# A graph-network kernel on five engines: issuing every engine's work in the kernel's own list order instead of the framework's own order

## The chip, the cores and the metric

The kernel runs on one core of a Trainium2 chip. The metric is the device time of one execution in microseconds (us), the median of several. Five engines take part: TensorE (PE in the profile; its weight loads are PEld), VectorE (DVE), ScalarE (ACT), GpSimd (POOL) and SyncE (SP), which issues the transfers. The profile lists each engine's instructions apart (in the kernel before 7664 on TensorE, 3479 on VectorE, 1802 on ScalarE, 519 on GpSimd), and shows for an engine's idle time the operation of another engine, or the transfer, that ended it (18.0 us of TensorE's ended with the gate L465 on ScalarE).

## The reference

A batch of 64 graphs with 256 nodes and 128 features, one 256x256 adjacency `adj`, float32. Four layers, each followed by a residual and a layer normalization. Cut to what matters:

```python
# layer 0: five steps of a gated recurrence (m_in = m_out because both matrices are adj)
def step(h):
    m = einsum('nm,bmd->bnd', adj, h);  av = concat([m, m]);  u3 = h @ u3_w.T + u3_b
    z = sigmoid(av @ w3_w.T + w3_b + u3)
    r = sigmoid(av @ w4_w.T + w4_b + u3)
    hv = tanh(av @ w5_w.T + w5_b + (r * h @ u5_w.T + u5_b))
    return (1 - z) * h + z * hv
# layer 1: edge values in a softmax (the same for all graphs), then adj-like @ (x @ W)
# layer 2: attention: softmax of scores per graph, masked by adj; then an MLP with two normalizations and relus
# layer 3: Chebyshev sums adj @ x, adj @ adj @ x with seven weights
x = layernorm(x + layer_k(x, adj))      # for k = 0..3
```

## The kernel before

Two graphs form a pair, there are 32 pairs, and each passes through a long chain of small dependent operations. To keep TensorE busy, the kernel weaves the chains of several pairs together: in the 1500 us of the middle TensorE is 95% busy, in the last 182 us, where few pairs are left, 78%. It does this with a scheduler of its own, written in Python and run while the program is built. Each operation is noted with the engine (or two possible engines), a duration, and what it reads and writes:

```python
SEEN = {"PE": 0.3, "ACT": 0.15, "DVE": 0.15, "POOL": 0.2, "SP": 2.5}   # the list's own figures: us until others see the end
DUE, LAST_DUE, LAST = 50.0, 10.0, 7                                   # pairs become due every 50 us, the last 7 every 10
...
def pool(us, fn, r, w):
    S.add([("POOL", us, fn)], r, w)
...
# Schedule.order: always the operation that can start first; among equals the most urgent pair
key = (start + (us if len(op.ways) > 1 else 0.0), self.due(op.pair) - op.rest, op.number)
...
return [(op, fn) for _, _, op, fn in sorted(out, key=lambda x: x[:2])]
```

I call the result the **list order**. It also decides which buffer each value gets. There are two sorts of operations in it. The *chain* of the recurrence sits between matmuls of the same pair:

```python
act(0.69, ... nc.scalar.activation(r, t, AF.Tanh, ...))       # L465, first gate; L471 and L479 are its sisters
dve(0.74, ... nc.vector.scalar_tensor_tensor(r, r, 1.0, hT))  # L467
dve(0.76, ...)  # L481     dve(0.74, ...)  # L482     dve(0.72, ... new state)  # L484
evacuate(...)   # L180 on ACT or L181 on DVE: a finished PSUM bank to SBUF
```

The *side work* comes from layers 1 to 3 and the normalizations of all layers. Some of it is four instructions under one entry of the list:

```python
def stats(y):                                   # bn_stats x4, bn_aggr x4 on DVE (L426, L428): 1.75
    pool(0.23, ... add eps)  # L431/L433        pool(1.04, ... pow -0.5)  # L434
    dve(0.16, ...)                              # L436: -mean * rstd
def normalize(y, o):                            # four ACT (L447, 1.85) or four DVE (L442, 1.45) instructions
...
for c in range(4): act(0.51, ... AF.Prelu)      # L550, softmax scores
for c in range(4): act(0.69, ... AF.Exp)        # L553, with a sum
pool(1.3, ... hg + gat_b)                       # L573
act-or-dve(0.62 / 0.8, ... Relu)                # L574
```

At the end of the kernel the list is emitted, one call after the other. In the kernel before, the framework receives these calls and schedules them again: it may give each engine another order, as long as data dependencies hold.

Of the kernel before, what the change touches and what calls it, by code (L numbers as in the profile page):

```python
# [153 lines left out]
def kernel(ctx: ExitStack, tc: tile.TileContext, x, xT, adj, adjT, mats, cols, rows, out):  # L154
# [6 lines left out]
    S = Schedule(n_pairs)  # L161
# [468 lines left out]
    tiles = {}  # L630
    for cls, (n, count) in CLASSES.items():
        where = {"PS": psum, "D": dram}.get(cls, shared)
        tiles[cls] = [where.tile([1, n] if cls == "D" else [P, n], F32, name=f"{cls.lower()}{k}") for k in range(count)]
    for op, fn in S.order(tiles):
        for v, ap in op.tiles.items():
            v.ap = ap
        fn()


# [39 lines left out]
```

## Time and profile before

| | before |
|---|---|
| time, median of 3 | 1832.84 us (1828.77 to 1836.44) |
| profiled span, mean TensorE clock | 1831.8 us, 0.986 |

What TensorE needs if it never waits is worked out in the prediction: about 1656 us. What lies above that is waiting, and time in which the granted clock was 0.50 (47.8 us of it fall within the matmuls). The views that the prediction reads are shown there. A list of waits shows for which operation of which other engine an engine stood still. The columns of a list of waits are the line that waited, the line waited for, then the total in us, how often, and the longest.

```profile
ACT a L574 <- POOL a L573: 80.8, 25, 4.6
ACT a L447 <- DVE s L436: 66.2, 33, 6.6
ACT x L447 <- DVE s L436: 62.2, 33, 5.1
ACT b L550 <- DVE s L542: 33.3, 24, 3.4
```

ScalarE stood 242.5 us (the sum of the four) in front of side work that was not ready.

### The profile page before, as it was taken

What the parts mean: (1) busy time and instruction counts of PE and PEld (TensorE: products, weight loads), DVE (VectorE), ACT (ScalarE), POOL (GpSimd) and SP (SyncE); (2) the same over time, 40 slices, a digit from 0 to 9 for tenths busy, and PEclk for the clock granted to TensorE, in tenths of its full rate; (3) what the DMA queues carried; (4) which work ended last, traced back from release to release, by engine and by line L of the source; (5) the groups of instructions that cost most, each with busy time, mean ns of one, the idle gap of its engine ahead of it and who ended that gap; (6) DMA issues with size and microseconds to landing.
All of it is one profiled execution on the core that took longest, in us unless ns stands there. A gap on an engine that the chain in (4) does not pass through costs nothing. (4 is left out here: it accounts for less than half of the span.)

```text
span 1831.8 us, 22230 instructions
## 1 busy us (share of the span) xinstructions
PE 1707.2 (93%) x7664; PEld 1197.9 (65%) x7664; DVE 1158.6 (63%) x3479; ACT 870.2 (48%) x1802; POOL 442.8 (24%) x519
## 2 busy tenths in 40 slices
PE   8999999999999899999998999999899999998886
PEld 5666667666766566766666666676665666666775
DVE  5467657567566656565665665666666665766764
ACT  3445344545455544444555453454453445444653
POOL 0013112212231312221232221222212220215342
PEclk9999999999999999999999999999999999999999
DMA  5000000010001000000000001001000000000000
GB/s 148 6 12 12 18 24 18 18 30 12 18 24 29 1 30 18 24 12 23 12 23 18 18 18 29 18 18 27 3 18 12 17 13 1 6 18 6 13 24 24
DMA packets 48978, 37.36 MB, mean 20 GB/s; under 512 B 2912, under 2 KB 44384, under 8 KB 48864
## 3 DMA queue, kind: packets, MB, share of 16 engines
q1 hardware_dynamic: 48864, 35.93, 6.7%
q8 instruction: 60, 0.98, 0.2%
q14 instruction: 54, 0.44, 0.1%
HBM read 27.47 MB, written 8.45 MB: 20 GB/s over the span
## 5 line engine op out<-in xcount | busy, mean ns | idle before, releaser
L180 ACT COPY a<-ps 128x512 f32<-128x512 f32 (+1 forms) x508 | 267.4, 537 | 346.9 <-PE ps L412 210.3
L431 POOL TENSOR_SCALAR s<-s 128x4 f32<-128x4 f32 x160 | 52.0, 325 | 1018.0 <-DVE s L428 949.5
L412 PE MATMUL ps<-aT,a 128*128 128x256 f32 x1024 | 250.0, 384 | 6.9 <-ACT a L180 6.5
L412 PEld LDWEIGHTS ps<-aT,a 128*128 128x128 f32 x1024 | 189.8, 192 | 59.6 <-issue 23.3
L434 POOL TENSOR_TENSOR s<-s,neg_half 128x4 f32<-128x4 f32 x192 | 204.7, 1066 | 15.8
L469 PE MATMUL ps<-a,w 128*128 128x512 f32 x320 | 165.5, 605 | 18.0 <-ACT a L465 18.0
L479 ACT ACTIVATE a<-ps,bzrh 128x512 f32<-128x512 f32 x160 | 109.3, 684 | 144.2 <-PE ps L477 142.9
L426 DVE BATCH_NORM_STATS2 s<-a 128x6 f32<-128x128 f32 x640 | 141.4, 280 | 54.8 <-ACT a L180 52.6
L465 ACT ACTIVATE a<-ps,bzrh 128x512 f32<-128x512 f32 x160 | 109.1, 684 | 134.9 <-PE ps L462 134.8
L436 DVE SCALAR_TENSOR_TENSOR s<-s 128x4 f32<-128x4 f32 x192 | 40.7, 212 | 207.0 <-POOL s L434 206.7
L462 PE MATMUL ps<-a,w 128*128 128x512 f32 x320 | 164.9, 597 | 5.7 <-ACT a L180 5.7
L477 PE MATMUL ps<-a,u5h 128*128 128x512 f32 x320 | 165.0, 597 | 2.7 <-DVE a L467 2.7
L476 PE MATMUL ps<-a,w 128*128 128x512 f32 x320 | 165.7, 600 | 0.0
L481 DVE TENSOR_TENSOR a<-a,a 128x512 f32<-128x512 f32 x128 | 93.2, 728 | 103.1 <-ACT a L479 102.8
L500 PEld LDWEIGHTS ps<-W,a 128*128 128x128 f32 x1024 | 127.4, 192 | 41.5 <-issue 12.4
L500 PE MATMUL ps<-W,a 128*128 128x128 f32 x1024 | 132.8, 277 | 18.9 <-DVE a L507 6.8
L390 PEld LDWEIGHTS ps<-ident,a 128*128 128x128 f32 x768 | 93.0, 142 | 83.3 <-DVE a L484 37.8
L390 PE MATMUL ps<-ident,a 128*128 128x128 f32 x768 | 115.6, 276 | 29.4 <-DVE a L484 29.2
L467 DVE SCALAR_TENSOR_TENSOR a<-a,a 128x512 f32<-128x512 f32 x128 | 93.0, 728 | 75.9 <-ACT a L465 75.5
L471 ACT ACTIVATE a<-ps,bzrh 128x512 f32<-128x512 f32 x160 | 109.4, 684 | 57.7 <-PE ps L469 57.0
L412 PE MATMUL ps<-aT,x 128*128 128x256 f32 x512 | 127.4, 390 | 4.2 <-ACT x L447 3.5
L461 PE MATMUL ps<-a,W 128*128 128x512 f32 x256 | 131.2, 594 | 0.0
(146 smaller groups left out, 2826.2 us busy)
## 6 DMA issues: line engine op xcount, KB each, us to landing
t<-xT_in SPq DMA_DIRECT2D x32, 256.0 KB
x<-x_in SPq DMA_DIRECT2D x32, 256.0 KB
a<-d SPq DMA_DIRECT2D x32, 256.0 KB
y_out<-a SPq DMA_DIRECT2D x32, 256.0 KB
W<-mats_in SPq DMA_DIRECT2D x1, 832.0 KB
W<-mats_in SPq DMA_DIRECT2D x1, 512.0 KB
d<-a SPq DMA_DIRECT2D x32, 2.0 KB
rbc<-rows_in SPq DMA_DIRECT2D x1, 385.0 KB
```

Of the source, the lines that this page charges most:

```text
L180: S.add([("ACT", us_act, lambda: nc.scalar.copy(o(), i())), ("DVE", us_dve, lambda: nc.vector.tensor_copy(o(), i()))], r, w)
L390: nc.tensor.transpose(t.at(4, P)[:, c, :], x_like(i)[:, c, :], ident.ap)
L412: nc.tensor.matmul(t.at(2, N)[:, b, :], tokens(i)[:, 2 * b + j, :], right.ap[:, j, :], start=(j == 0), stop=(j == 1))
L426: nc.vector.bn_stats(st.at(4, 6)[:, c, :], tokens(y)[:, c, :])
L434: pool(1.04, lambda: nc.gpsimd.tensor_tensor(rs(), rs(), neg_half.ap, op=ALU.pow), [s, neg_half], [s])
L461: nc.tensor.matmul(t.at(512), mat("u3"), hT.at(512), start=True, stop=False)
L462: nc.tensor.matmul(t.at(512), w345.ap[:, 1, :], mT.at(512), start=False, stop=True)
L469: pe(mm(512), lambda t=t, mT=mT: nc.tensor.matmul(t.at(512), w345.ap[:, 0, :], mT.at(512), start=False, stop=True, skip_group_check=True), ...
L471: act(0.69, lambda t=t, z=z: nc.scalar.activation(z.at(512), t.at(512), AF.Tanh, bias=bzrh.ap[:, 0:1], scale=0.5), [t, bzrh], [z])
L476: nc.tensor.matmul(t.at(512), w345.ap[:, 2, :], mT.at(512), start=True, stop=False)
L477: nc.tensor.matmul(t.at(512), u5h.ap, r.at(512), start=False, stop=True)
L500: nc.tensor.matmul(tokens(t)[:, c, :], tokens(i)[:, c, :], w(), start=(k == 0), stop=(k == len(lefts) - 1))
```

## The change

The intent is to switch the framework's rescheduling off, so that each engine issues in exactly the list order. The operations, buffers and list stay the same.

```diff
-    for op, fn in S.order(tiles):
-        for v, ap in op.tiles.items():
-            v.ap = ap
-        fn()
+    with tc.manual_schedule():
+        for op, fn in S.order(tiles):
+            for v, ap in op.tiles.items():
+                v.ap = ap
+            fn()
```

## The prediction

> **What bounds the kernel now.** I read the page first, then the waits of TensorE, then single stretches of the timeline, and last the table by stage. The page:
>
> ```profile
> PE 1707.2 (93%) x7664; PEld 1197.9 (65%) x7664; DVE 1158.6 (63%) x3479; ACT 870.2 (48%) x1802; POOL 442.8 (24%) x519
> ...
> PE   8999999999999899999998999999899999998886
> ...
> L180 ACT COPY a<-ps 128x512 f32<-128x512 f32 (+1 forms) x508 | 267.4, 537 | 346.9 <-PE ps L412 210.3
> ```
>
> TensorE is the bound; DVE has 37% and ACT 52% of the span to spare. "93% busy" is not the floor, because matmul ends are modelled. I took the start-to-start times of neighbouring matmuls instead (the trace matches the built program one to one). Medians: a 512-column fp32 product (two records) 859 ns, 800 of them; 256 columns 432 ns, 1419; 128 or 130 columns 223 ns, 898; a transpose 109 ns, 1416. That is 687 + 613 + 200 + 154 + 1 for six tiny ones, about 1656 us. The span of 1831.8 is then 5.1 before the first matmul, 1656.3 of TensorE at its own pace, 7.8 after the last start, and 162.6 us of excess. No reordering can go under about 1669; the question is how much of the 162.6 it gives back.
>
> TensorE's own waits:
>
> ```profile
> PE ps L390 <- DVE a L484: 29.2, 18, 4.3
> PE ps L469 <- ACT a L465: 18.0, 16, 3.2
> PE ps L613 <- ACT a L180: 7.6, 7, 2.4
> ```
>
> TensorE waits for the next state of the recurrence (L484), for the first gate (L465) and for evacuated banks (L180), all from engines that are not full. Why are they late? One such wait in the timeline, ACT and then PE:
>
> ```profile
> 151.51 0.63 ACT L574 ACTIVATE a<-a 128x512 f32<-128x512 f32 x1 [3.02 <-DVE s L545]
> 152.05 0.49 ACT L550 ACTIVATE b<-b,h 128x256 f32<-128x256 f32 x1
> 152.45 0.67 ACT L479 ACTIVATE a<-ps,bzrh 128x512 f32<-128x512 f32 x1
> 153.02 1.29 ACT L550 ACTIVATE b<-b,h 128x256 f32<-128x256 f32 x3
> 154.22 0.67 ACT L465 ACTIVATE a<-ps,bzrh 128x512 f32<-128x512 f32 x1
> ...
> 150.18 1.02 PE L462 MATMUL ps<-a,w 128*128 128x512 f32 x2
> ...
> 154.94 1.13 PE L469 MATMUL ps<-a,w 128*128 128x512 f32 x2 [2.02 <-ACT a L465]
> ```
>
> The L465 needs only the L462 product, done at 151.2. It starts at 154.22, behind one L574 and four L550, all of which the kernel's list schedule places after it (its emission number is 923, theirs 925 and 939 to 946). The framework's scheduler let them in front; TensorE stood for 2.02 us.
>
> The end is a stage of its own:
>
> ```profile
> core 0: us, PE busy (x) PEld busy (x) DVE busy (x) ACT busy (x) POOL busy (x), PEclk, DMA share, GB/s
> ...
> 150.00:1650.00 1500.00, 1422.21 (x6322) 985.98 (x6321) 954.38 (x2809) 721.10 (x1480) 355.95 (x410) 0.99 0.06 18
> 1650.00:1832.00 182.00, 142.83 (x788) 120.00 (x786) 116.18 (x455) 88.47 (x220) 73.95 (x91) 0.92 0.06 17
> ```
>
> TensorE is 95% busy in the 1500 us of the middle and 78% in the last 182, at a lower granted clock: few pairs are left, and latency sets the pace.
>
> [...] at 154.22 a ready L465 stood behind others. So issue order is everything the change has to work with. [...] eleven stretches at half clock, each near 3.4 or 6.8 us, 54.3 us in all, 6.5 of them after the last matmul. Ten fall in the matmuls and can cost at most 47.8/2 = 24 us; the five in the middle part each begin close to a TensorE gap (near 209, 267, 640, 1175 and 1390 us; four of these gaps are 2.1 to 4.4 us long). [...] a 128x512 two-input operation is followed after 0.60 us by one that is not held, after 0.726 by one that waits for it. So each dependent neighbour costs 0.125 us, and order decides how many there are.
>
> **The change part by part.** The two built programs have the same instructions on the same buffers (4540 matmuls, 3479 DVE, 1672 ACT, 517 POOL after the preamble); only order and waits differ. Against emission order the old program steps backwards 27 times on PE, 276 on ACT and 506 on DVE; the new one never does on PE and DVE. So TensorE's order hardly changes; its producers' does. The four-part groups (L447, L442, L550, L553), which the framework spread out among others, become solid.
>
> Removed. 98 TensorE gaps over 0.3 us with a releaser hold 128.6 us (88 up to 1600 us, 40.5 after). For each I looked at what the releaser's engine ran between the arrival of its operands and its start. In 73 of 98 it ran work that the list places later: 55.7 us of the gaps directly, 76.5 us when I follow the releasers back to the preceding matmul (capped at each gap). Largest: L447 pieces 31.7, DVE L442 13.8, L553 10.4, L550 and L574 9.1 each (uncapped). I take the middle, 66, and 80% of it, because the moved work must still go somewhere: **-53 us**.
>
> Clock: if half of the middle stretches go with their gaps, half of 12 us: **-6**.
>
> Added. In 7 of those 98 cases the list puts work (17.7 us together) in front of the releaser that ran behind it before, and a list made with fixed durations stalls at an operation that is not ready: I put **+10**, a choice. At the start TensorE now takes L412 first, which waits for the adjacency (landed near 7.1 us), where before it did 1.7 us of L461 from 5.07: **+2**. On DVE, dependent neighbours go from 374 to 503, 129 x 0.125 = 16 us over a DVE with 670 us idle: mostly hidden, **0**. TensorE instructions with a wait go from 1336 to 1714; in the trace 256-column products with and without a wait both have a median of 432 ns: **0**.
>
> Sum: -53 - 6 + 10 + 2 = -47; 1832.8 - 47 = **1786 us**.
>
> **The rivals.** (a) Head-of-line stalls take the place of the overtaking. A greedy scheduler fills gaps; a frozen order does not. Eight ACT pieces (L550, L553) in a row are 4 x 0.40 + 4 x 0.49 = 3.6 us that a gate cannot enter. For it: the 37% of DVE. Against it: only 7 of 98 cases get new work in front. It would give 1815 to 1850. (b) The gaps are latency, not order: L481, L482, L484 are a chain of three dependent DVE operations whatever the order. For it: 52 of 128.6 us are not explained by overtaking, and after 1700 us hardly any is (4.5 of 26.5). It would give about 1810. (c) All overtaking and most clock loss go: -76 - 15, about 1742.
>
> **Range and chances.** Rival (c) with some stalls sets the low end, a good half of rival (b)'s way the high end: 1752 to 1815. Faster by 2% means under 1796.2, a gain of 37, less than the direct 55.7 alone: 0.70. Within 2%: 0.28. Slower than 1869 would need stalls far over what is removed: 0.02.
>
> **What would show it.** Right: TensorE's waits for L465 and L180 fall by more than half, L447 no longer ahead of a ready L465; waits for L484 fall less; fewer half-clock stretches in the middle; matmul medians unchanged. Wrong: ACT or DVE idle in front of an unready operation while a ready one stands behind it and TensorE waits; or the middle stays at 95% busy; or a tail longer than 182 us at the same work.

## The result

The changed kernel took **1719.85 us** (median of 4 runs, 1718.46 to 1720.10) against 1834.64 us for the kernel before in the same rounds (1828.77 to 1837.94). The ratio is **0.9376**, with a 95% interval of 0.9350 to 0.9402. Here and below, a ratio is the mean time of one kernel's fast runs over that of the other's of the same rounds, so it is not quite the ratio of the medians quoted. The gain of 115 us is more than twice the predicted 47, and the time is below the predicted range of 1752 to 1815. A second measurement in other rounds (e16 below) gave 0.9391.

The page of the changed kernel: first the busy time of each engine, its share of the span and its instructions; then TensorE and its clock in 40 slices (a digit is tenths); then the shares of the chain of work that ended last; and last the evacuations on ScalarE, as the prediction showed them (busy time, mean ns of one; idle before them and what ended it).

```profile
PE 1676.0 (98%) x7664; PEld 1196.0 (70%) x7664; DVE 1177.8 (69%) x3479; ACT 881.9 (51%) x1802; POOL 449.7 (26%) x519
...
PE   8999999999999999999999999999999999998796
...
PEclk9999999999999999999999999999999999999898
...
PE 93%; DVE 3%; POOL 2%; ACT 1%; issue 1%; DMA 0%; SPq 0%; POOLq 0%; DVEq 0%
...
L180 ACT COPY a<-ps 128x512 f32<-128x512 f32 (+1 forms) x508 | 268.5, 539 | 393.9 <-PE ps L412 241.5
```

All slices of the middle are full. The chain that ended last is TensorE's own work for 93% of the span. One evacuation takes 539 ns (537 before), so it did not become quicker in itself. The table by stage shows the same; its stages start at 150 us and break at 1540:

```profile
core 0: us, PE busy (x) PEld busy (x) DVE busy (x) ACT busy (x) POOL busy (x), PEclk, DMA share, GB/s
150.00:1540.00 1390.00, 1388.75 (x6311) 983.44 (x6310) 964.74 (x2791) 727.23 (x1469) 360.25 (x404) 1.00 0.07 19
1540.00:1718.00 178.00, 145.78 (x802) 119.94 (x800) 127.03 (x475) 93.83 (x230) 78.43 (x95) 0.93 0.06 19
```

TensorE is busy for 1388.75 of 1390 us. In the same 1390 us the kernel before completed 5862 matmul records, this one 6311. The last 178 us still look as before: TensorE is 82% busy at a clock of 0.93.

What TensorE still waits for, from its waits:

```profile
PE ps L412 <- DMA aT<-adjT_in: 8.3, 1, 8.3
PE ps L293 <- ACT b L553: 6.8, 4, 6.1
PE ps L469 <- ACT a L465: 1.0, 2, 0.8
PE ps L390 <- DVE a L484: 0.9, 2, 0.6
PE ps L613 <- ACT a L180: 0.3, 1, 0.3
```

The three waits that led the list before, 29.2 for L484, 18.0 for L465 and 7.6 for L180, are down to 0.9, 1.0 and 0.3. What is left is the first transfer and one gap near the end. In the timeline of ScalarE and then TensorE (start, length, operation; in brackets the idle time before it and what ended that):

```profile
1589.60 1.70 ACT L550 ACTIVATE b<-b,h 128x256 f32<-128x256 f32 x4 [1.69 <-DVE s L542]
1594.56 0.51 ACT L553 ACTIVATE b<-b,s 128x256 f32<-128x256 f32 x1 [3.26 <-DVE s L547]
...
1595.21 2.38 PE L293 MATMUL ps<-ident,b 128*128 128x128 f32 x8 [6.09 <-ACT b L553]
```

Here few pairs are left. The softmax of one pair has to run from end to end, and TensorE, whose next operation in the list is the L293 behind it, stands for 6.09 us. Whether another order could have filled this gap, this view does not show; e15 below has a list without it.

And this is ScalarE's list of waits, the same four lines as shown of before:

```profile
ACT b L550 <- DVE s L542: 8.1, 8, 1.7
ACT a L574 <- POOL a L573: 7.0, 11, 2.2
ACT x L447 <- DVE s L436: 3.0, 2, 2.2
ACT a L447 <- DVE s L436: 1.3, 2, 0.9
```

From 242.5 us to 19.4. VectorE's largest wait on side work (L436 for the power on GpSimd, L434) went from 206.7 to 58.2 us. **In the framework's order the two producers of TensorE stood still in front of side work that was not ready yet, with ready chain work behind it.** In the list order, side work stands later and is ready when its turn comes: between 150 and 1500 us a group of L447 on ScalarE now starts 6.36 us after its last input was written (mean, from the trace and the program's dependencies), where it started after 0.29. The gate L465 starts after 0.26, where it started after 0.69.

The span fell by 113.5 us. From start to start of every matmul, it divides so:

| term | before, us | after, us | difference | predicted |
|---|---|---|---|---|
| TensorE gaps over 0.3 us with a releaser (98, then 31) | 128.6 | 32.1 | -96.5 | -53 and +10 |
| cost of half-clock stretches within the matmuls (at most half their length) | 24 | 10 | -14 | -6 |
| first matmul | 5.07 | 8.27 | +3.2 | +2 |
| after the last start | 7.8 | 8.1 | +0.3 | 0 |
| rest: small gaps and rounding, what is left to the span | | | -6.5 | 0 |

For each gap I then looked, in a second pass, at what the releasing engine did between the arrival of its operand and its own start. "Overtaken" is time in which it ran work that the list places later. "In list order" is time in which it ran other work. "Stall" is time in which it stood idle in front of an unready operation. "Operand late" is the part in which the operand itself was still to come. Where a wait held more than one of these, the gap is shared among them in proportion. This second pass sums to within about 1 us of the gaps above.

| TensorE gap by what its releaser did, us | before | after |
|---|---|---|
| overtaken | 37.4 | 0 |
| in list order | 14.2 | 6.5 |
| stall | 38.4 | 3.6 |
| operand late | 39.7 | 22.2 |

The stalls of before were L574 in front of an unready L573 (11.3), L447 in front of L436 (9.8), L436 in front of L434 on VectorE (9.1) and L550 in front of L542 (2.7), with smaller ones. They weigh as much as the overtaking. "Operand late" is only this releaser's own view: when each operand is followed back, through the operations that made it, to the preceding matmul, the gaps of before divide into 50.0 us of overtaking, 44.4 of stall, 25.2 of list-order work and 8.6 that the operations themselves take; after the change it is 0, 3.9, 15.5 and 12.7.

### The profile page after: what moved, and what is told of

The parts are those of the page before. It is cut to its first block, busy times and chain, and to the rows that moved or that the text cites. A ratio compares the mean times of both kernels' runs of the same rounds, so it can differ in the third digit from the quotient of the medians.

```text
span 1718.3 us, 22198 instructions
## 1 busy us (share of the span) xinstructions
PE 1676.0 (98%) x7664; PEld 1196.0 (70%) x7664; DVE 1177.8 (69%) x3479; ACT 881.9 (51%) x1802; POOL 449.7 (26%) x519
## 4 chain that ended last, share of the span: by engine, by line
PE 93%; DVE 3%; POOL 2%; ACT 1%; issue 1%; DMA 0%; SPq 0%; POOLq 0%; DVEq 0%
PE ps L412 24%; PE ps L469 8%; PE ps L461 8%; PE ps L476 8%; PE ps L462 8%; PE ps L477 8%; PE ps L390 7%; PE ps L500 6%; PE ps L567 3%; PE ps L605 3%; PE ps L606 3%; PE ps L613 3%; PE ps L524 2%; PE ps L293 2%; POOL s L434 1%
## 5 line engine op out<-in xcount | busy, mean ns | idle before, releaser
L180 ACT COPY a<-ps 128x512 f32<-128x512 f32 (+1 forms) x508 | 268.5, 539 | 393.9 <-PE ps L412 241.5
L412 PE MATMUL ps<-aT,a 128*128 128x256 f32 x1024 | 246.0, 379 | 0.7 <-ACT a L180 0.7
L412 PEld LDWEIGHTS ps<-aT,a 128*128 128x128 f32 x1024 | 188.1, 190 | 47.7 <-issue 26.1
L434 POOL TENSOR_TENSOR s<-s,neg_half 128x4 f32<-128x4 f32 x192 | 215.8, 1124 | 15.8
L479 ACT ACTIVATE a<-ps,bzrh 128x512 f32<-128x512 f32 x160 | 109.9, 687 | 171.0 <-PE ps L477 168.7
L465 ACT ACTIVATE a<-ps,bzrh 128x512 f32<-128x512 f32 x160 | 109.3, 686 | 166.8 <-PE ps L462 166.8
L476 PE MATMUL ps<-a,w 128*128 128x512 f32 x320 | 163.5, 593 | 0.0
L462 PE MATMUL ps<-a,w 128*128 128x512 f32 x320 | 163.4, 592 | 0.0
L469 PE MATMUL ps<-a,w 128*128 128x512 f32 x320 | 161.8, 593 | 1.0 <-ACT a L465 1.0
L481 DVE TENSOR_TENSOR a<-a,a 128x512 f32<-128x512 f32 x128 | 89.5, 700 | 92.9 <-ACT a L479 92.3
L467 DVE SCALAR_TENSOR_TENSOR a<-a,a 128x512 f32<-128x512 f32 x128 | 91.4, 717 | 89.0 <-ACT a L465 88.9
L412 PE MATMUL ps<-aT,x 128*128 128x256 f32 x512 | 126.2, 388 | 11.9 <-DMA aT<-adjT_in 8.3
L482 DVE SCALAR_TENSOR_TENSOR a<-a,a 128x512 f32<-128x512 f32 x160 | 118.5, 741 | 22.5 <-ACT a L471 18.0
L412 PEld LDWEIGHTS ps<-aT,x 128*128 128x128 f32 x512 | 96.8, 195 | 38.7 <-issue 13.2
```

The costliest lines, as they stand in the source:

```text
L180: S.add([("ACT", us_act, lambda: nc.scalar.copy(o(), i())), ("DVE", us_dve, lambda: nc.vector.tensor_copy(o(), i()))], r, w)
L412: nc.tensor.matmul(t.at(2, N)[:, b, :], tokens(i)[:, 2 * b + j, :], right.ap[:, j, :], start=(j == 0), stop=(j == 1))
L434: pool(1.04, lambda: nc.gpsimd.tensor_tensor(rs(), rs(), neg_half.ap, op=ALU.pow), [s, neg_half], [s])
L462: nc.tensor.matmul(t.at(512), w345.ap[:, 1, :], mT.at(512), start=False, stop=True)
L469: pe(mm(512), lambda t=t, mT=mT: nc.tensor.matmul(t.at(512), w345.ap[:, 0, :], mT.at(512), start=False, stop=True, skip_group_check=True), ...
L476: nc.tensor.matmul(t.at(512), w345.ap[:, 2, :], mT.at(512), start=True, stop=False)
```

## The experiments

The theory when they began: the whole effect is the issue order, and the larger part of it is that side work issued too early holds up the ready work behind it on the same engine (in the prediction's timeline the gate L465 starts at 154.22, 3.0 us after its product was done at 151.2, behind one L574, one L479 and four L550). The rivals were these. The manual schedule changes something besides the order (e1). One engine's order, ScalarE's, carries it (e2 to e4). It is a matter of side work being too early, curable by moving it later (e5, e6, e8). It is the four-part groups that are now solid (e8, e9). The list wins because its durations are right (e7, e10 to e12), or the framework's scheduler loses with any list (e13, e14).

For e1 to e6 and e8 I needed any order on any engine. The kernel takes down its engine calls in list order and reissues them, manually scheduled, in a permutation that is stored in the file. All permutations respect the data dependencies. The common edit:

```diff
-    nc = tc.nc
+    nc = Recorder(tc.nc)          # takes down each engine call
...
-    with tc.manual_schedule():
-        for op, fn in S.order(tiles):
-            ...
-            fn()
+    for op, fn in S.order(tiles):
+        ...
+        fn()                      # only taken down
+    with tc.manual_schedule():
+        for k in order_of(len(nc.calls)):   # the stored permutation of 10371 calls
+            nc.issue(k)
```

All results (median and range of 4 runs; the ratio is against the kernel before of the same rounds, for which the median lay between 1831.27 and 1834.64). The last two columns are idle time from the lists of waits: ScalarE in front of L574, L447 and L550 (the four lines above, summed; in e9 and e15 the lines are numbered otherwise), and VectorE's L436 in front of L434.

| run | time, us | ratio [95%] | ACT idle | DVE idle |
|---|---|---|---|---|
| before | 1834.64 | 1 | 242.5 | 206.7 |
| changed | 1719.85 | 0.9376 [0.9350, 0.9402] | 19.4 | 58.2 |
| e1 framework's order on all, manual | 1834.99 (1828.41-1841.31) | 1.0012 [0.9982, 1.0043] | 242.6 | 207.1 |
| e2 framework's order on ScalarE only | 1909.30 (1908.24-1911.23) | 1.0418 [1.0400, 1.0437] | 279.5 | 51.8 |
| e3 on VectorE only | 1791.00 (1780.96-1795.15) | 0.9765 [0.9730, 0.9799] | 11.6 | 202.6 |
| e4 on TensorE only | 1728.03 (1726.41-1728.57) | 0.9428 [0.9413, 0.9442] | 24.4 | 59.3 |
| e5 framework's order, ScalarE side work later | 1891.54 (1890.08-1894.59) | 1.0326 [1.0301, 1.0351] | 79.2 | 289.1 |
| e6 changed, L574 earlier | 1752.37 (1749.82-1754.25) | 0.9560 [0.9533, 0.9586] | 78.5 | 54.8 |
| e7 list made with GpSimd at a quarter | 1748.39 (1746.19-1749.78) | 0.9542 [0.9519, 0.9564] | 82.4 | 169.7 |
| e8 changed, ScalarE groups pulled apart | 1853.04 (1850.38-1853.70) | 1.0111 [1.0087, 1.0135] | 66.1 | 113.9 |
| e9 list with split groups | 1716.86 (1715.63-1717.41) | 0.9369 [0.9345, 0.9393] | 51.0 | 71.0 |
| e10 list with all side work at a quarter | 2056.04 (2054.43-2057.55) | 1.1219 [1.1194, 1.1243] | 306.1 | 224.6 |
| e11 list with durations near the trace | 1717.13 (1715.33-1720.60) | 0.9372 [0.9349, 0.9394] | 30.5 | 59.5 |
| e12 e11 with another end | 1714.11 (1713.12-1715.39) | 0.9353 [0.9333, 0.9374] | 26.0 | 60.2 |
| e13 list of e10, framework's scheduler | 1975.33 (1973.51-1976.59) | 1.0780 [1.0753, 1.0806] | 279.4 | 245.7 |
| e14 list of e12, framework's scheduler | 1812.66 (1811.07-1814.53) | 0.9893 [0.9872, 0.9914] | 203.9 | 204.5 |
| e15 split, measured, other end | 1706.97 (1706.02-1708.38) | 0.9316 [0.9297, 0.9335] | 43.9 | 69.4 |
| e16 changed kernel again | 1720.80 (1720.11-1721.54) | 0.9391 [0.9373, 0.9410] | 19.4 | 58.2 |

### e1: the framework's order, issued manually

```diff
+ORDER = ...   # the order of the program before, on all five engines
```

> All five engines issue in the framework's order, taken from the built program of the kernel before, but by manual scheduling; the built program has the same instructions, order and waits on every engine as before (1336 TensorE instructions with a wait, as before). Theory O (issue order is all there is to it): 1830 to 1840 us, TensorE waits near 118 us again. Rival M (manual scheduling brings something besides the order): clearly under 1820 us.

It gives 1834.99 us, a ratio of 1.0012: the same as before. Its page repeats the busy times of before within 8 us:

```profile
PE 1714.6 (93%) x7664; PEld 1201.3 (65%) x7664; DVE 1157.9 (63%) x3479; ACT 870.1 (47%) x1802; POOL 443.2 (24%) x519
```

So, to within the 0.4% of the interval, manual scheduling does nothing besides the order, and the 115 us are the order.

### e2, e3, e4: one engine in the framework's order

```diff
+ORDER = ...   # e2: ScalarE near the framework's order, the other four in list order (247 steps back against the list; the program before has 276)
+ORDER = ...   # e3: VectorE (504 steps back; before 506)
+ORDER = ...   # e4: TensorE (26 steps back; before 27)
```

> List order on PE, DVE, POOL and SP exactly as in the changed kernel; ScalarE as near to the framework's order as the other engines allow (247 steps back against the list, 276 in the kernel before). Theory O with my own count of the overtakers (55 of 71 us of overtaking in front of TensorE's gaps was on ACT, 78%): 78% of the 115 us come back, 1810 us, waits of L465 and L180 first. Rival D (the gain came from the DVE chain L481, L482, L484): under 1750 us.

> Only VectorE in the framework's order (504 steps back against the list), all others as in the changed kernel. Theory O: the DVE share of the counted overtaking, 22% of 115 us, 1745 us. Rival D: 1790 us or more. If the two engines' effects do not add up to 115 us, a queue on one engine is late because of the other.

> Only TensorE in the framework's order (26 steps back against the list), all others as in the changed kernel. Theory O, in which TensorE's own order hardly matters: 1718 to 1728 us. Rival P (the 27 displaced matmuls carry the part of the gaps that I could not explain by overtaking, some 40 us): 1750 us or more.

TensorE's order costs 8 us over the 1720 of the changed kernel, and only in the last 200 us. VectorE's costs 71 and ScalarE's 189. The three sum to 268, where all engines together cost 115. Two of the three expectations missed. I had put e2 near 1810, and it came out slower than the kernel before. I had put e3 at 1745; its 1791 is the value of rival D, that the gain came from VectorE's chain L481, L482, L484. But rival D asked for e2 under 1750, so it does not hold alone either. One line of ScalarE's waits and two of TensorE's show how:

```profile
ACT b L550 <- DVE s L542: 102.5, 30, 5.7
```

```profile
PE ps L412 <- ACT a L180: 36.3, 13, 6.5
PE ps L469 <- ACT a L465: 31.3, 13, 7.4
```

ScalarE takes up L550 as early as in the framework's order, while VectorE computes its operand as late as in the list. The wait is 102.5 us, where it was 33.3 before and 8.1 after the change. The evacuations and gates behind it are late, and TensorE stands. An engine's order is good or bad only together with the orders of the others.

### e5: the framework's order with ScalarE's side work later

```diff
+ORDER = ...   # before's order; on ScalarE L447, L550, L553, L574 never before their place in the list: 2.2 places later on average
```

> The framework's order on all engines, with one difference: on ScalarE the side work (L447 normalization, L550 and L553 softmax, L574 relu) moves later towards its list place, by 2.2 places in the mean, as far as the other engines' order allows; the gates and evacuations keep their sequence. Theory H (side work issued too early blocks ScalarE, either by running in front of a ready gate or by standing unready at the head of the queue): a good part of the 115 us comes back, 1765 to 1800 us, and ScalarE's idle time in front of L574 falls from 81 us to under 40. Rival V (the loss is on VectorE or spread over all engines): over 1815 us.

I expected 1765 to 1800, since this takes away the early side work that stalls ScalarE (over 1815 if the loss is on VectorE or spread over all engines). It does that: ScalarE's idle time falls from 242.5 to 79.2 us. The kernel still slowed down to 1891.54 us, which is slower than before, and neither theory had that. Two lines show where it went, VectorE's wait and the first of TensorE's:

```profile
DVE s L436 <- POOL s L434: 289.1, 178, 11.1
```

```profile
PE ps L390 <- DVE a L484: 49.6, 17, 11.6
```

GpSimd now gets its operands later (its L509 waits 150.0 us for L447, where it had been 41.9), and VectorE, whose order had been left alone, stands in front of L436 for 289.1 us, where it had been 206.7. The stall moved to the next engine. So "side work earlier than it is ready" describes the kernel before, but moving it back on one engine is no cure.

### e6 and e8: the changed kernel with one piece of ScalarE's order moved

```diff
+ORDER = ...   # e6: list order, 29 of the L574 on ScalarE at their place in the framework's order: 5.5 places earlier on average
+ORDER = ...   # e8: list order, the parts of each L447, L550 and L553 group pulled apart by later work on ScalarE
```

> The changed kernel with 29 relus (L574) put on ScalarE where the framework had them, 5.5 places earlier in the mean; nothing else moves. They wait for GpSimd. Theory H: ScalarE idles in front of L574 for some 60 to 90 us (7 us in the changed kernel, 81 before) and TensorE pays some 15 to 25 of it: 1735 to 1745 us. Rival B (only the busy time of overtakers counts, 29 x 0.63 = 18 us on an engine that is half idle): under 1726 us.

> The changed kernel with the four-part groups on ScalarE (L447, L550, L553) pulled apart again: the pieces are put between the gates that follow, never earlier than in the list. Rival S (that groups stay solid is what helps): 1750 us or more. Theory H: splitting alone is harmless, 1715 to 1730 us in the middle part unchanged; the last 180 us may grow a little since the side work ends later there.

In e6 29 instructions of about 0.6 us, moved on a single engine, cost 33 us (1752.37 against 1719.85; I had expected 1735 to 1745). ScalarE's wait in front of them:

```profile
ACT a L574 <- POOL a L573: 65.5, 27, 3.6
```

It was 7.0 after the change. The other four engines keep the list order. The running time of the moved instructions, 29 x 0.63 = 18 us, could not cost 33 us even if TensorE paid all of it, so head-of-line stalling is a cause: 58.5 us more idle time on an engine that is 51% busy goes with 33 us more in a TensorE-bound kernel.

e8 asks whether the solid groups help or hurt. I expected no harm or a small gain (1715 to 1730). It took 1853.04 us, in the range of rival S (1750 or more). The moved parts, and what stood behind them, came late: TensorE waited 33.8 us for L574 and 30.4 for L553. It again moves a single engine against a plan that the others keep, so it says nothing on solid groups in a plan made for split ones. That is e9.

### e7: a list made with wrong durations for GpSimd

```diff
     def pool(us, fn, r, w):
-        S.add([("POOL", us, fn)], r, w)
+        S.add([("POOL", us / 4, fn)], r, w)
```

> Manual scheduling with a list that is made as if GpSimd were four times as fast; groups stay solid. Theory W (a frozen order is only as good as the durations it is made with; the framework's order looks like one made with too short a GpSimd): ScalarE and VectorE stall in front of operations that wait for GpSimd (L574, L447, L436), TensorE's gaps return, 1760 to 1830 us. Rival S (solid groups and manual order help whatever the durations): under 1735 us.

1748.39 us: 29 more than the changed kernel, less than the 1760 to 1830 that I expected. The wait for L573 on ScalarE is back at 52.8 us and VectorE's on L434 at 169.7. This is still a plan for all five engines, with one engine's durations wrong.

### e9: a list with the normalization as four operations

```diff
-        S.add([("ACT", 1.85, by_act), ("DVE", 1.45, by_dve)], [y, s], [o])
+        for c in range(4):
+            S.add([("ACT", 0.47, lambda c=c: ...), ("DVE", 0.37, lambda c=c: ...)], [y, s], [o])
```

> Manual scheduling; the list itself takes each four-part normalization as four operations, so it may put gates and other work between the parts, on the same plan for all engines. The last experiments showed that parts moved on one engine alone cost 30 to 190 us; theory C (what counts is that the five queues follow one plan) says that splitting inside one plan is harmless: 1705 to 1735 us. Rival S (solid groups are what helps): over 1760 us.

1716.86 us, a ratio of 0.9369 against the 0.9376 of the changed kernel in other rounds: the same. That the normalization groups became solid is neither the gain nor a loss. (The list also chose ScalarE for 116 instructions that had been on VectorE; the softmax groups L550 and L553 were not split in a plan by any run.) ScalarE's idle time rose to 51.0 us without harm; this fits idle time costing only where ready chain work stands behind and TensorE has used up its lead.

### e10, e11, e12: lists with other durations

```diff
 # e10: each also divided by 4: GpSimd, stats 1.75, normalize 1.85/1.45, Prelu 0.51, Exp 0.69, Relu on ACT 0.62
+        dve(1.75 / 4, fn, [y], [st, s])
 # e11: near the durations of the trace
+        dve(1.2, fn, [y], [st, s])                                 # stats, was 1.75
+        S.add([("ACT", 1.65, by_act), ("DVE", 1.15, by_dve)], ...)  # was 1.85 / 1.45
+            act(0.4, ... AF.Prelu)   # was 0.51
+            act(0.5, ... AF.Exp)     # was 0.69
+        evacuate(..., 0.5, 0.62)     # was 0.6, 0.68
 # e12: e11 and
-DUE, LAST_DUE, LAST = 50.0, 10.0, 7
+DUE, LAST_DUE, LAST = 50.0, 7.0, 8
```

> Manual scheduling with a list made as if all side work (GpSimd, normalizations, statistics, softmax parts, relus) took a quarter of its time; still one plan for all five queues. Theory W (the framework's loss is that of a plan with wrong durations): 1790 us or more, with ScalarE's normalizations in front of ready gates again. Theory C alone (one plan, whatever its durations): under 1760 us, like the run with only GpSimd too short (1748).

> Manual scheduling with the list's durations closer to the issue intervals of the trace (normalization 1.65 and 1.15 us, softmax parts 0.4 and 0.5, statistics 1.2, evacuation 0.5 and 0.62). The middle of the changed kernel is already at TensorE's own pace (2.4 us of excess in 1400 us), so only the last 180 us, with some 40 us of excess, can gain: 1700 to 1715 us. If a plan with shorter durations brings stalls: 1720 to 1740 us.

> As the run before, and the last pairs pushed a little earlier (LAST_DUE 7 for 10, LAST 8 for 7): the last 180 us gain or lose 5 to 10 us, 1695 to 1715 us; the middle is unchanged.

e10 is the slowest kernel of all, 2056.04 us. The changed durations also move 59 instructions from VectorE to ScalarE, since the list chooses the engine; against 336 us that is little, but it is in the number. ScalarE's waits and the first of TensorE's:

```profile
ACT a L574 <- POOL a L573: 136.3, 31, 6.7
ACT a L447 <- DVE s L436: 87.3, 39, 6.4
ACT x L447 <- DVE s L436: 74.0, 45, 3.6
```

```profile
PE ps L412 <- ACT a L574: 113.9, 27, 7.1
```

The three lines of ScalarE are those that led before the change, and larger. TensorE's line is another: before, it waited 0.6 us for L574, and here the late side work itself holds it up. So theory C alone (one plan for all five queues, whatever its durations: under 1760 us) is refuted: a plan that believes side work to be short puts it too early, and a frozen order pays for it. In the other direction there is little to win: e11 gives 1717.13 us (0.9372; expected 1700 to 1715), the same as the changed kernel, although the author's durations were up to 0.55 us off. From 1500 us on it leaves 27 us above TensorE's own pace in place of 40, but it has 13 us between 150 and 1500 in place of 2. e12 gains 3 us more, with an interval that overlaps that of e11. The list was already good enough.

### e13 and e14: the same lists under the framework's scheduler

```diff
-    with tc.manual_schedule():
-        for op, fn in S.order(tiles): ...
+    for op, fn in S.order(tiles): ...
```

> The list with side work at a quarter of its time (2056 us when frozen), now under the framework's scheduler as in the kernel before. If the framework makes its own plan and takes from the list only buffers and ties: 1800 to 1900 us. If it inherits the list's order: over 1980 us.

> The list of e12 (1714 us when frozen) under the framework's scheduler. If the loss is the framework's own plan, it is there again: 1810 to 1850 us. If the durations in the list were what the framework lacked: under 1780 us.

The bad list of e10 becomes better under the framework, 1975 against 2056 us (0.961 of it, from the two ratios). The good list of e12 becomes worse, 1813 against 1714 us (1.058). e14's ScalarE waits, with the list of e12, in which they were 2.9 and 11.8 us:

```profile
ACT a L447 <- DVE s L436: 67.2, 37, 4.7
ACT a L574 <- POOL a L573: 60.0, 22, 5.9
```

e14 came out as expected of a loss that is the framework's own. e13 fitted neither of its expectations: with a plan of the framework's own it should have taken 1800 to 1900 us, with the list's order over 1980. Its 1975 us are close to the second, and the wait that leads on TensorE is that of e10, 64.0 us for L574 where it was 113.9. So the framework does not replace the list; it reworks it, and inherits much of it. It repairs part of the poor list and spoils the good one, by the stalls that the kernel before shows. e14 against before (0.9893) also says that the better list helps somewhat even then.

### e15 and e16: the best of it, and the changed kernel again

```diff
 # e15: e12, and the four-part normalization of e9 with 0.42 (ACT) and 0.29 (DVE) for a part
```

> Manual scheduling with separate parts, durations near the trace's and the last pairs a little earlier, all together: the middle stays at TensorE's pace, the end gains a few us over e9 (1717) and e12 (1714): 1705 to 1715 us.

> The changed kernel again, beside e15 on the same chip: 1718 to 1722 us.

e15 takes 1706.97 us, e16 1720.80 in the same rounds: 0.992 of it (0.9316 over 0.9391; the intervals of the two do not overlap). It is faster than both kernels. The gain lies at the end: over TensorE's own pace there are 16 us from 1500 us on, where the changed kernel has 40. The middle did not stay at TensorE's pace, as I had expected: TensorE is busy for 1341.39 of the 1350 us between 150 and 1500, against 1348.75. This list also runs 100 more instructions on ScalarE instead of VectorE, so the order is not all that differs. The mean clock is 0.999, and the slices of TensorE and its clock show no thin place but the first and the last slice:

```profile
PE   7999999999999999999999999999999999999998
...
PEclk9999999999999999999999999999999999999999
```

## Why the prediction was wrong

The direction, the bound and the mechanism "order alone" were right. The size was not: -115 for -47.

- **The step that failed is "Removed": it put only 53 us of the gaps on order, and had no term for engines standing idle at unready side work.** It took the 128.6 us of TensorE gaps, counted as removable only the time in which a releasing engine *ran* work that the list places later, and kept 80% of that. The 52 us that overtaking did not explain were left in place, as latency of the kind of rival (b). The second pass is stricter about overtaking in the releasing engine itself (37.4 us, where the prediction had 55.7, because a gap that also held a stall is shared) and finds beside it 38.4 us in which that engine stood idle before unready side work. This stall had no term in the sum at all: asking what an engine was *running* cannot find time in which it ran nothing. Of the 96.5 us of gaps that the change removed, overtaking is 37.4 and stall 34.8 (38.4 to 3.6); the rest is operands that had been late further back (39.7 to 22.2) and list-order work (14.2 to 6.5). Followed back to the preceding matmul, only 8.6 us of all the gaps are time that the operations themselves take, where the prediction had left 52 to latency; 44.4 are stall.
- **"+10" for new stalls had the wrong sign as a net term.** I assigned head-of-line stalls to the new order, because "a greedy scheduler fills gaps; a frozen order does not". The trace of before had the contradiction: 242.5 us of ScalarE idle in front of L574, L447 and L550, against 19.4 after. New stalls within TensorE gaps are 3.6 us. A scheduler that fills gaps while the program is being built still produces a fixed order for the chip (e1 issues that order manually, at 1.0012 of the time of before), and it too depends on how well its durations and its look ahead fit. So the stalls of rival (a) were real and belonged to the kernel before; e6 shows their price and e10 shows that a list order can have them as well.
- **Rival (b), latency, fails in the middle; at the end it is open.** Between 150 and 1540 us TensorE is busy for 1388.75 of 1390. From 1500 us on there are 40 us of excess over TensorE's own pace, out of 45.6 in all; before, the time from 1600 us on had 52 of 162.6. So the change did little there, as the prediction said. That it is latency whatever the order is not shown: the list of e15 leaves 16 us there in place of 40.
- **Rival (c), 1742, came nearest** and was still 22 us too slow, for the same reason: it is all of the overtaking, but none of the stalls.
- **Clock, -6:** right in kind, wrong in size, about -14. The half-clock stretches within the matmuls went from 47.8 us to 20.5, and none is left in the middle, whose gaps are gone too; the first, of 13.7 us, came at 1590.9 us, in the gap of 6.09 us. I had let half of the middle stretches stay. What decides is not shown: close to the five in the middle of the kernel before (3.4 or 6.8 us long), the longest idle times of TensorE in the records were 3.2, 1.9, 2.7, 1.2 and 4.3 us, while nine other gaps of 2.0 to 2.7 us before 1400 us had none close by.
- **Start, +2:** it was +3.2, TensorE's first matmul now starting at 8.27 with L412, when the adjacency is there. (In the trace of before, the last part of that transfer landed at 7.61 us, where the prediction has 7.1, and L412 started at 7.75.)
- **Dependent neighbours on VectorE, 0, and more TensorE waits, 0:** right. VectorE's busy time rose from 1158.6 to 1177.8, which is 69% of the span; a 256-column product still has a median of 432 ns, and TensorE instructions with a wait rose from 1336 to 1715 (the prediction's 1714 was one short).
- **What would show it:** four signs came as written. Waits for L465 and L180 fell by more than half, L447 no longer runs in front of a ready L465 (28.3 us in 27 cases before, none after), there are fewer half-clock stretches in the middle, and the medians did not move. One was wrong: waits for L484 did not "fall less", they fell from 29.2 to 0.9. L484 ends a chain of three, but the chain was late by order: followed back to the preceding matmul, the 32.2 us of gaps that L484 ended before hold 17.9 us of overtaking, most of it on VectorE, and 8.6 of stall, nearly all of it VectorE in front of L436 (e3, with VectorE alone in the framework's order, brings the wait back to 31.5).

What stays open: why the framework places side work so early. Lists with durations that are too short give the same waits on ScalarE (e7, e10), though not on TensorE, whose longest wait there is for L574; durations that are too small in the framework's own plan could explain it, but no run shows what it assumes, and its rules for ties would do as well. How much of the 115 us falls to which engine can't be said either, because single engines do not add up (e2 to e4). The orders of GpSimd and SyncE changed too (31 and 12 steps back in the program before, none after), and neither was tried alone.

## What to carry to other kernels

When several engines feed a full one, look at the idle time of the *feeding* engines in front of unready work, even where they are half empty: in e6, 58.5 us more of it on a ScalarE that had been 51% busy went with 33 us more in all. Here a plan for all engines that was roughly right (one duration was off by about half, 1.75 for 1.2) was worth issuing unchanged; moving one engine's order against it cost 8 to 189 us in five tries (e2, e3, e4, e6, e8). If the durations may be far off, try the framework's scheduling too: in the one such pair here it gave 1975 us for a list that gave 2056 when it was frozen.
